# A graph layer whose table rows come by indirect gathers: row fetches per group 16 to 22, two kinds of loads moved from SyncE to ScalarE, the table's end and one buffer moved forward

## The chip, the cores and the metric

The kernel runs on one core of a Trainium2 chip. Its metric is the device time of one execution in microseconds (us). Before the change three runs took 2118.93, 2115.63 and 2113.80 us, median 2115.63. The profile comes from one more execution, which took 2117.82 us.

## The reference

N = 12500 nodes with D = 128 features, E = 212500 edges sorted by destination, 8 heads of 16. Per edge, rows of two projections of the source node are multiplied with a projection of the destination node and with a projection of the edge's attributes:

```python
Q = (x @ WQ).reshape(N, H, dh); K = (x @ WK).reshape(N, H, dh); V = (x @ WV).reshape(N, H, dh)
Eh = (edge_attr @ WE).reshape(-1, H, dh)
score = K[src] * Q[dst] / jnp.sqrt(jnp.float32(dh)) * Eh
score = jnp.exp(jnp.clip(score.sum(-1, keepdims=True), -5.0, 5.0))
wV = jax.ops.segment_sum(V[src] * score, dst, num_segments=N)
Z = jax.ops.segment_sum(score, dst, num_segments=N)
h = x + (wV / (Z + ATTN_EPS)).reshape(N, D)
...
x = _layernorm(x + batchnorm(h) * bn_gamma + bn_beta)   # in the reference spelled out
```

## The kernel before, in words

**Tiles and groups.** The edges are cut into 1661 tiles of 128. A *window* is 4 tiles and a *group* is two windows, 8 tiles; there are 208 groups, and the last one has 5 tiles. One pass of the main loop (line 783) is called iteration g below. It finishes group g and prepares the groups up to g+5.

**The table.** `kvd` in DRAM holds a row of 256 floats (K and V side by side, 1 KB) for every node. `table_rows` (line 669) computes it in 25 steps of 4 blocks of 128 nodes: TensorE multiplies, ScalarE and VectorE take turns at copying out of PSUM, SyncE stores. Groups 0 to 7 do not use the table. Their rows of `x` are gathered (64 gathers) while the table is built and are projected by TensorE: groups 0 to 2 during the table, groups 3 to 7 in `project_main` (line 493), one in each of iterations 2 to 6. From group 8 on, GpSimd gathers the rows of `kvd`, one indirect DMA for each tile (line 225). The first of these waits until the whole table is stored.

**Steps beside the table.** `steps` (line 701) is a list written out by hand that hands work of the first groups out over the table's steps, from step 8 on. Its last entries, `ehqe(0)`, `both_halves(0)`, `turn_back(0)`, `q_mm(2)`, `q_hi(2)` and `q_mid(2)`, fall on the table's steps 21 to 23. `ehqe` multiplies the edge attributes (TensorE, copied out by ScalarE) and spreads Q over the edges (TensorE); `both` multiplies the two (VectorE); `turn_back` transposes the product so that edges lie on the partitions.

**Slots.** A *slot* is 8 KB in each partition and holds one group's table rows. Slots 0 to 7 exist from the start: 0 to 3 first hold x rows of two groups each, 4 to 6 hold the projected rows of groups 0 to 2. A ninth slot (NSLOT) is made at the end of iteration 7 (lines 832 to 836), when the pool `table` (four buffers of 4 KB by partition, line 495 and line 670) is closed. When `message(g)` has read a slot it is free, and `load_kv` (line 279) puts the next group's gathers into `queued`; they are issued in the next iteration, the first of them after TensorE's step of that iteration (`pace`, line 236). So from group 17 on, group k's gathers wait for iteration k-9 at the earliest.

**Rows by SyncE.** In some groups the eighth tile is not gathered by GpSimd. SyncE fetches its 128 rows one at a time: `fetch_rows` (line 268) loads the byte offsets into registers (line 270, one load for all of the iteration's rows) and issues one 1 KB DMA per row (line 277). `ROW_STREAMS` says 16 rows an iteration, from iteration 8 to 199; `row_plan` (line 58) turns that into 24 groups (18, 26, 34, ... 202), each used three iterations after its last row was issued. Such a group has 7 gathers in place of 8.

**What else SyncE issues**, in program order at the start of each iteration: `load(g+4)` (line 490), the edge attributes `ea`, 512 KB, three buffers; below group 16 `load_rel` (line 401), two DMAs of edge places turned along the free axis, one set for each group; from group 16 on `load_quad` (line 388), two DMAs `rbq` of 256 KB for four groups at once, every fourth iteration; then the rows. ScalarE issues only the loads at the start and the stores of turned places (line 380), which `place` makes for 64 windows at a time.

**Who waits for whom among direct DMAs.** The trace's records of SyncE's and ScalarE's direct DMAs show that each carries one of eight semaphores (numbers 100 to 105, 107 and 118), handed round in the program's order over both engines, and that each waits on its own semaphore before it is issued: DMA number n waits until DMA number n-8 has landed, whichever of the two engines issued that one.

**ScalarE in one iteration**, in order: `clip_exp(g)` (lines 607 and 608), `q_hi`, `x_out`, `sums_out`, `q_window`, the two copies of `ehqe(g+2)` (line 562), `q_mid(g+3)` (line 550). After that it waits for the next group's scores.

Of the kernel before, what the change touches and what calls it, by code (L numbers as in the profile page):

```python
# [8 lines left out]
F32 = mybir.dt.float32  # L9
# [8 lines left out]
P = 128  # L18
# [3 lines left out]
G = 8  # L22
U = 4
WN = 64
CH = 512
NSLOT = 8
# [3 lines left out]
ROWS = P  # L30
FIRST_ROW = 8
ROW_LAG = 3
ROW_STREAMS = (("SP", 16),)
RQ = 4


# [46 lines left out]
def gnn_kernel(  # L83
# [19 lines left out]
    nc = tc.nc  # L103
# [3 lines left out]
    usizes, ustarts, cuts, due, _ = plan(N, T)  # L107
    NG = NW // 2
# [8 lines left out]
    rows = ctx.enter_context(tc.tile_pool(name="rows", bufs=1))  # L117
# [5 lines left out]
    tab = tps.enter_context(tc.tile_pool(name="table", bufs=1))  # L123
    late = []
# [85 lines left out]
    free = list(range(NSLOT))  # L210
    pending = list(range(nxg, NG))
# [1 line left out]
    steady = [False]  # L213

    def slot(i):
        return (rows if i < NSLOT else late[0]).tile([P, 2 * G * P], F32, name=f"slot{i}")

    def kv_view(g, t):
        SLOT[g] = t[0]
# [9 lines left out]
    queued = []  # L229
# [18 lines left out]
    for (_, n), groups in zip(ROW_STREAMS, row_plan(usizes)):  # L248
# [6 lines left out]
        if tot % n:  # L255
            q = tot // n
# [22 lines left out]
    def load_kv():  # L279
        while free and pending and table[0]:  # L280
            g = pending.pop(0)
            i = free.pop(0)
            kv_view(g, (i, slot(i)))
            for j in range(sizes[g] - (g in by_row)):
                queued.append((gather, KV[g](j, j + 1, 0, 2 * P).rearrange("p a d -> p (a d)"), kvd,
                               starts[g] + j))
            if not steady[0]:
                issue()

    for g in range(nxg):  # L290
        if g % 2 == 0:
            PAIR[g // 2] = free.pop(0)
            t = slot(PAIR[g // 2])
# [41 lines left out]
    def within(f, g):  # L335
        return f(g) if 0 <= g < NG else None
# [47 lines left out]
    def load_quad(q):  # L384
        t = late[0].tile([P, RQ, U * P], BF16, name="rbq", bufs=2)
        for h in (0, 1):
            at = ustarts[2 * RQ * q + h] * P
            nc.sync.dma_start(t[h * WN:(h + 1) * WN], bass.AP(
                tensor=relT.tensor, offset=relT.offset + at, ap=[[0, WN], [G * P, RQ], [1, U * P]]))
        for k in range(RQ):  # L390
            RB[RQ * q + k] = t[:, k, :]

    quads = range(-(-2 * FIRST_ROW // RQ), sizes.count(G) // RQ)
# [90 lines left out]
    def halves(g):  # L484
        return [(0, usizes[2 * g]), (usizes[2 * g], nt(g))]

    def load(g):
        n = nt(g)
        EA[g] = wp.tile([P, G, P], F32, name="ea", bufs=3)
        nc.sync.dma_start(EA[g][:, :n, :].rearrange("p a b -> p (a b)"),  # L490
                          eaT[:, starts[g] * P:(starts[g] + n) * P])

    def project_main(g):

        half = [tab.tile([P, 4, 2 * P], F32, name="t", bufs=4) for _ in range(2)]
        KV[g] = lambda a, b, c, n=P: half[a // 4][:, a % 4:a % 4 + b - a, c:c + n]
        turn_x(g, 0, True)
        turn_x(g, 4, True)
        yield
        for a in (0, 4):  # L500
            project(g, a, lambda: turned().rearrange("p (a b) d -> p a (b d)", b=2), True)
            yield
# [36 lines left out]
    def q_mm(g):  # L539
        PQ[g] = small_ps[:, 0, :]  # L540
        return nc.tensor.matmul(PQ[g], XW[g], w_q, start=True, stop=True)  # L541

    def q_hi(g):
        Q3[g] = wp.tile([P, 3, P], BF16, name="q3", bufs=2)
        nc.scalar.activation(Q3[g][:, 0, :], PQ[g], AF.Copy, scale=0.25)

    def q_mid(g):
        QR[g] = wp.tile([P, P], F32, name="qr", bufs=1)
        nc.vector.scalar_tensor_tensor(QR[g], PQ[g], 0.25, Q3[g][:, 0, :], op0=OP.mult, op1=OP.subtract)
        nc.scalar.activation(Q3[g][:, 1, :], QR[g], AF.Copy)  # L550
# [4 lines left out]
    def ehqe(g):  # L555

        QE[g], WT[g] = [], []
        for a, b in halves(g):
            eh = psp.tile([P, U * P], F32, name="ps_e", bufs=2)[:, :(b - a) * P]
            nc.tensor.matmul(eh, w_e, EA[g][:, a:b, :].rearrange("p a b -> p (a b)"), start=True, stop=True)  # L560
            t = wp.tile([P, U * P], F32, name="wt", bufs=2)
            nc.scalar.activation(t[:, :(b - a) * P], eh, AF.Copy)  # L562
            WT[g].append(t)
            QE[g].append(psp.tile([P, U * P], F32, name="ps_q", bufs=2)[:, :(b - a) * P])
        for k in range(3):
            for h, (a, b) in enumerate(halves(g)):
                r = slice(h * WN, (h + 1) * WN)
                nc.tensor.matmul(QE[g][h], Q3[g][r, k, :], OT[g][r, :(b - a) * P], start=(k == 0), stop=(k == 2))  # L568
# [6 lines left out]
    def turn_back(g):  # L575

        PW[g] = []
        for h, (a, b) in enumerate(halves(g)):
            ps = turned()
            for j in range(b - a):  # L580
                nc.tensor.transpose(ps[:, j, :], WT[g][h][:, j * P:(j + 1) * P], ident)  # L581
            PW[g].append(ps)
# [84 lines left out]
    NB = -(-N // P)  # L667

    def table_rows(b):
        t = tab.tile([P, 4, 2 * P], F32, name="t", bufs=4)  # L670
        for q in range(b, min(b + 4, NB), 2):
            ps = wide()
            m = min(2, NB - q)
            for i in range(m):
                n = min(P, N - (q + i) * P)
                nc.tensor.matmul(ps[:n, i, :], hx[:, (q + i) * P:(q + i) * P + n], w_kv, start=True, stop=True)
            fl = min(m, N // P - q)
            if fl:
                step = evac(t[:, q - b:q - b + fl, :], ps[:, :fl, :])
            if fl < m:  # L680
                nc.vector.tensor_copy(t[:n, q - b + fl, :], ps[:n, fl, :])
        full = min(4, N // P - b)
        if full > 0:
            nc.sync.dma_start(kvd[b * P:(b + full) * P, :].rearrange("(c p) d -> p c d", p=P), t[:, :full, :])
        if b + 4 > N // P and N % P:
            r0 = N // P * P
            nc.sync.dma_start(kvd[r0:N, :], t[:N - r0, N // P - b, :])
        while len(queued) > max(0, nxg * G - 11 - 12 * (b // 4 + 1) // 5):
            pace(step)

    NQ = -(-NB // 4)
# [4 lines left out]
    def both_halves(g):  # L696
        both(g, 0)
        both(g, 1)
# [2 lines left out]
    steps = [[(locate,)], [(place, runs[0])], [], [(q_mm, 0), (q_hi, 0)],  # L701
             [(q_mid, 0), (load_rel, 0)], [(q_lo, 0), (load, 0)], [(q_mm, 1), (q_hi, 1), (load_rel, 1)],
             [(q_mid, 1)], [(q_lo, 1), (load_rel, 2)], [(load, 1)], [(turned_onehot, 0)],
             [(turned_onehot, 1)], [], [(ehqe, 0), (both_halves, 0)], [(turn_back, 0), (q_mm, 2), (q_hi, 2)],
             [(q_mid, 2)]]
    first_step = NQ - len(steps) - 1
    assert first_step > 3 and max(piece) < first_step + 14
    windows = {first_step + 2: (0, 1), first_step + 8: (2,)}
    for q in range(NQ):
# [5 lines left out]
        for g, a in piece.get(q, []):  # L715
            if a == 0:
                i = free.pop(0)
# [11 lines left out]
        f(*a)  # L729
    table[0] = True  # L730
    load_kv()
    ehqe(1)
    onehot(0)
    within(load, 2)
# [2 lines left out]
    q_window(3)  # L737
    load_rel(4)
    load(3)


    done = set()
# [38 lines left out]
        attn(g)  # L781

    for g in range(NG - 2):
        within(load, g + 4)
        within(load_rel, g + 5)
        if (g + 6) % RQ == 0 and (g + 6) // RQ in quads:
            load_quad((g + 6) // RQ)
        fetch_rows(g)
        within(products, g)
        within(both_halves, g + 1)  # L790
        step = within(add_x, g - 3)
        step = within(q_mm, g + 3) or step
        if step is not None and queued and g >= FIRST_ROW:
            pace(step)
        issue()
        within(gather_sum, g - 1)
        if g + 1 < nxg and g + 1 not in SLOT:
            for _ in project_main(g + 1):
                pass
        within(turn_back, g + 1)  # L800
        within(scores, g)
        within(clip_exp, g)
        within(q_hi, g + 3)
        within(x_out, g - 3)
        within(sums_out, g - 1)
        within(q_lo, g + 2)
        within(denom, g - 2)
        within(recip, g - 2)
        within(attn, g - 2)
        within(q_window, g + 4)  # L810
        within(turned_onehot, g + 3)
        within(ehqe, g + 2)
        within(q_mid, g + 3)
        within(message, g)
        within(onehot, g + 1)
        if g == 2:
            load_last()
        for r in runs[1:]:
            if g == max(4, r[0] // 2 - 12):
                place(r)  # L820
        within_checks(g)
        if NSLOT in free and not pending:
            free.remove(NSLOT)
        while free and todo and not pending:
            load_x()
        bn_parts(2 * g - 5, 2 * g - 3)
        if g == NG - 5:
            assert done >= set(range(NPRE))
            norm_first()
        if g == 4:  # L830
            nc.vector.tensor_scalar(row_ids, row_ids, 8 * P, None, op0=OP.mult)
        if g == FIRST_ROW - 1:
            tps.close()
            late.append(tps.enter_context(tc.tile_pool(name="late", bufs=1)))
            free.append(NSLOT)
            load_kv()
    last = NG - 1
# [327 lines left out]
```

## Time and profile before

| | before |
|---|---|
| runs, median (lowest to highest), us | 2115.63 (2113.80 to 2118.93) |
| profiled execution, us | 2117.82 |
| its span, from first to last instruction, us | 2116.0 |
| what lies around the span, us | 1.8 |
| busy: TensorE, VectorE, ScalarE, GpSimd | 80%, 77%, 30%, 75% |
| gathers of x and of the table on GpSimd | 64 and 1573 |
| rows fetched by SyncE | 3072 |
| bytes moved, mean rate | 386.83 MB, 183 GB/s |

The busy shares are averages over the whole span. [...] SyncE has no busy share at all, since issuing DMAs is not counted; its time is read from the timeline of its own queue. A line of the timeline gives the start, the time from the first to the last instruction of the merged row, the engine (SPq is SyncE's queue), line, operation, tiles, how many, and in brackets how long the engine stood idle before and who ended that.

### The profile page before, as it was taken

Reading aid. Unit: us, or ns where it says so; the run is one execution under the profiler, and the core shown is the slowest. Engines: PE = TensorE matmul, PEld = TensorE weight load, DVE = VectorE, ACT = ScalarE, POOL = GpSimd, SP = SyncE. Lnnn points to the kernel's source line nnn. Section 1 sums busy time; section 2 is a strip of 40 time slices with the busy share of each in tenths; the row PEclk is TensorE's granted clock in tenths of the full one; section 3 lists DMA queues with packets and bytes.
Section 4 is the critical chain, followed back from the end, with each engine's and each line's share of the span. In section 5 each row is a group of like instructions: output and inputs, shape, how many; then the busy total and the mean of one; then the engine's idle time right before and its main releaser. Section 6 shows DMA issues by size and latency. Waiting matters only on the chain. (4 is left out here: it accounts for less than half of the span.)

```text
span 2116.0 us, 37688 instructions
## 1 busy us (share of the span) xinstructions
PE 1694.3 (80%) x9414; PEld 1103.1 (52%) x9414; DVE 1633.9 (77%) x3601; ACT 635.2 (30%) x2480; POOL 1581.2 (75%) x1673
## 2 busy tenths in 40 slices
PE   8899888887777777787877787878787788787877
PEld 6565555555454445455554554455455455454557
DVE  3559989997787787787777777777777778778777
ACT  2343333332232232222222232322222223223225
POOL 7776777777777777777777777777777777777775
PEclk9999999999999998999999999988999998999989
DMA  8856656666566555566565566565566555564674
GB/s 295 289 184 177 187 175 191 188 190 193 158 187 186 167 175 169 157 187 188 167 180 162 159 186 188 168 178 163 165 186 181 176 172 161 168 189 144 184 264 128
DMA packets 177913, 386.83 MB, mean 183 GB/s; under 512 B 38862, under 2 KB 94711, under 8 KB 177687
## 3 DMA queue, kind: packets, MB, share of 16 engines
q0 software_dynamic: 77552, 210.48, 33.9%
q1 hardware_dynamic: 95972, 171.08, 26.5%
q10 hardware_dynamic: 4163, 2.79, 0.4%
q8 instruction: 77, 1.26, 0.2%
q14 instruction: 149, 1.22, 0.2%
HBM read 364.58 MB, written 19.63 MB: 182 GB/s over the span
## 5 line engine op out<-in xcount | busy, mean ns | idle before, releaser
L225 POOL DMA_INDIRECT slot<-kvd,srcs x1573 | 1492.4, 949 | 487.5 <-issue 414.5
L631 PE MATMUL ps_a<-msg,oh 128*128 128x136 f32 (+1 forms) x3322 | 553.1, 308 | 1.7 <-DVE msg L616 1.7
L592 DVE TENSOR_TENSOR p<-slot,ps_t 128x512 f32<-128x512 f32 (+1 forms) x406 | 267.9, 673 | 323.6 <-DMA slot<-kvd,srcs 250.1
L631 PEld LDWEIGHTS ps_a<-msg,oh 128*128 128x128 f32 (+1 forms) x3322 | 447.6, 177 | 86.3 <-issue 61.7
L560 PE MATMUL ps_e<-ea,w_e 128*128 128x512 f32 x832 | 438.8, 654 | 27.7 <-DMA ea<-eaT 26.0
L607 ACT ACTIVATE ps_m<-s 128x64 f32<-128x64 f32 (+1 forms) x209 | 47.5, 227 | 1243.7 <-DVE s L606 931.4
L581 PE MATMUL ps_t<-ident,wt 128*128 128x128 f32 x1661 | 251.2, 293 | 118.0 <-DVE wt L573 116.4
L656 PE MATMUL ps_m<-ident,at 128*128 128x128 f32 x412 | 97.7, 320 | 227.8 <-DVE oh L524 222.9
L581 PEld LDWEIGHTS ps_t<-ident,wt 128*128 128x128 f32 x1661 | 196.3, 148 | 150.5 <-DVE wt L573 143.1
L573 DVE TENSOR_TENSOR wt<-wt,ps_q 128x512 f32<-128x512 f32 x416 | 265.6, 680 | 8.4 <-PE ps_q L568 7.2
L562 ACT ACTIVATE wt<-ps_e 128x512 f32<-128x512 f32 x416 | 233.5, 586 | 65.7 <-PE ps_e L560 61.8
L598 DVE TENSOR_REDUCE s<-p 128x64 f32<-128x1024 f32 (+1 forms) x209 | 251.9, 1205 | 0.1
L616 DVE TENSOR_TENSOR msg<-slot,ps_m 128x1024 f32<-128x1024 f32 (+1 forms) x205 | 242.2, 1182 | 1.4 <-ACT ps_m L607 1.0
L560 PEld LDWEIGHTS ps_e<-ea,w_e 128*128 128x128 f32 x832 | 158.9, 212 | 149.3 <-issue 110.7
L656 PEld LDWEIGHTS ps_m<-ident,at 128*128 128x128 f32 x412 | 63.6, 194 | 319.7 <-ACT q L550 297.1
L568 PE MATMUL ps_q<-ot,q 64*128 64x512 bf16 x1248 | 174.0, 385 | 0.0
L568 PEld LDWEIGHTS <-q 64*128 64x128 bf16 x1248 | 44.5, 95 | 196.7 <-issue 172.6
L521 DVE TENSOR_TENSOR oh<-ps_m,rel_i 128x512 f32<-128x512 f32 x208 | 142.0, 683 | 0.0
L510 ACT ACTIVATE xw<-hx 128x64 f32 x416 | 83.9, 248 | 66.4 <-issue 53.2
L661 ACT ACTIVATE hx<-ps_m 128x64 f32 x412 | 90.4, 219 | 8.0 <-PE ps_m L657 1.2
L647 DVE SCALAR_TENSOR_TENSOR at<-os,keep,rz 128x128 f32<-128x128 f32 x208 | 73.2, 352 | 25.1 <-PE ps_m L656 1.5
L541 PE MATMUL ps_m<-w_q,xw 128*128 128x128 f32 x416 | 86.2, 291 | 1.0 <-ACT xw L510 0.9
(172 smaller groups left out, 1553.7 us busy)
## 6 DMA issues: line engine op xcount, KB each, us to landing
ea<-eaT SPq DMA_DIRECT2D x207, 512.0 KB
byrow<-kvd SPq DMA_DIRECT2D x3072, 1.0 KB
slot<-kvd,srcs POOLq DMA_INDIRECT x1573
rbq<-relT SPq DMA_DIRECT2D x94, 256.0 KB
kvd<-t SPq DMA_DIRECT2D x24, 512.0 KB
slot<-xT SPq DMA_DIRECT2D x24, 256.0 KB
out<-o SPq DMA_DIRECT2D x23, 256.0 KB
hx<-xT SPq DMA_DIRECT2D x11, 512.0 KB
```

The costliest lines, as they stand in the source:

```text
L225: return nc.gpsimd.indirect_dma_start(out=out, out_offset=None, in_=table, in_offset=bass.IndirectOffsetOnAxis(ap=srcs[:, e:e + 1], axis=0))
L521: nc.vector.tensor_tensor(one, iota_ps[:, None, :].to_broadcast([P, n, P]), r[:, :n, None].to_broadcast([P, n, P]), op=OP.is_equal)
L560: nc.tensor.matmul(eh, w_e, EA[g][:, a:b, :].rearrange("p a b -> p (a b)"), start=True, stop=True)
L562: nc.scalar.activation(t[:, :(b - a) * P], eh, AF.Copy)
L568: nc.tensor.matmul(QE[g][h], Q3[g][r, k, :], OT[g][r, :(b - a) * P], start=(k == 0), stop=(k == 2))
L573: nc.vector.tensor_tensor(t, t, QE[g][h], op=OP.mult)
L581: nc.tensor.transpose(ps[:, j, :], WT[g][h][:, j * P:(j + 1) * P], ident)
L592: nc.vector.tensor_tensor(PR[g][:, c:d, :], KV[g](c, d, 0), PW[g][i][:, c - a:d - a, :], op=OP.mult)
L598: nc.vector.tensor_reduce(SS[g][:, a:b, :], PR[g][:, a:b, :].rearrange("p t (h d) -> p t h d", d=DH), axis=AX.X, op=OP.add)
L616: nc.vector.tensor_tensor(MSG[g][:, a:b, :P].rearrange("p t (h d) -> p t h d", d=DH), KV[g](a, b, P).rearrange("p t (h d) -> p t h d", d=D ...
L631: nc.tensor.matmul(AGG[g][WN if j >= n else 0:], OH[g][j], MSG[g][:, j, :], start=(j == 0), stop=(j == n - 1))
L656: nc.tensor.matmul(ps, AT[g], ident, start=True, stop=False)
```

## The change

`ROW_STREAMS` goes from 16 to 22 rows an iteration. SyncE no longer issues `ea` and `rbq` in the loop: ScalarE does, at the end of its work in iteration g, for group g+5 and one iteration earlier for the quads; SyncE loads group 4 ahead of the loop. The steps of group 0 and the Q of group 2 are taken out of the table's steps and stand behind the table. The ninth slot is made at the start and serves as two of the table's four buffers; it is freed for gathers at the end of iteration 6 in place of 7. The first gathers of iterations 8 to 11 no longer wait for TensorE's step.

```diff
-ROW_STREAMS = (("SP", 16),)
+ROW_STREAMS = (("SP", 22),)
...
-        return (rows if i < NSLOT else late[0]).tile([P, 2 * G * P], F32, name=f"slot{i}")
+        return rows.tile([P, 2 * G * P], F32, name=f"slot{i}")
+
+    first = slot(NSLOT).rearrange("p (h c d) -> p h c d", h=2, d=2 * P)
+
+    def table_tile(q):
+        return first[:, q % 4] if q % 4 < 2 else tab.tile([P, 4, 2 * P], F32, name="t", bufs=2)
...
-            nc.sync.dma_start(t[h * WN:(h + 1) * WN], bass.AP(
+            nc.scalar.dma_start(t[h * WN:(h + 1) * WN], bass.AP(
...
-    def load(g):
+    def load(g, by=nc.sync):
...
-        nc.sync.dma_start(EA[g][:, :n, :].rearrange("p a b -> p (a b)"),
+        by.dma_start(EA[g][:, :n, :].rearrange("p a b -> p (a b)"),
...
-        half = [tab.tile([P, 4, 2 * P], F32, name="t", bufs=4) for _ in range(2)]
+        half = [table_tile(2 * (g % 2) + a) for a in (0, 1)]
...
-        t = tab.tile([P, 4, 2 * P], F32, name="t", bufs=4)
+        t = table_tile(b // 4)
...
-             [(turned_onehot, 1)], [], [(ehqe, 0), (both_halves, 0)], [(turn_back, 0), (q_mm, 2), (q_hi, 2)],
-             [(q_mid, 2)]]
-    first_step = NQ - len(steps) - 1
+             [(turned_onehot, 1)]]
+    first_step = NQ - len(steps) - 5
...
     load_kv()
+    ehqe(0)
+    q_mm(2)
+    q_hi(2)
+    both_halves(0)
+    q_mid(2)
+    turn_back(0)
     ehqe(1)
...
     load(3)
+    load(4)
...
     for g in range(NG - 2):
-        within(load, g + 4)
         within(load_rel, g + 5)
-        if (g + 6) % RQ == 0 and (g + 6) // RQ in quads:
-            load_quad((g + 6) // RQ)
         fetch_rows(g)
...
-        if step is not None and queued and g >= FIRST_ROW:
+        if step is not None and queued and g >= FIRST_ROW + 4:
             pace(step)
...
         within(q_mid, g + 3)
+        if g + 5 < NG:
+            load(g + 5, nc.scalar)
+        if (g + 7) % RQ == 0 and (g + 7) // RQ in quads:
+            load_quad((g + 7) // RQ)
         within(message, g)
...
-        if NSLOT in free and not pending:
-            free.remove(NSLOT)
...
             late.append(tps.enter_context(tc.tile_pool(name="late", bufs=1)))
+        if g == FIRST_ROW - 2:
             free.append(NSLOT)
             load_kv()
```

## The prediction

> **What bounds the kernel now.** I read the page's groups first. All sums are made against the profiled execution (2117.82 us: span 2116.0 and 1.8 around it), which lies 2.2 us above the median of the runs, 2115.63.
>
> ```profile
> L225 POOL DMA_INDIRECT slot<-kvd,srcs x1573 | 1492.4, 949 | 487.5 <-issue 414.5
> L592 DVE TENSOR_TENSOR p<-slot,ps_t 128x512 f32<-128x512 f32 (+1 forms) x406 | 267.9, 673 | 323.6 <-DMA slot<-kvd,srcs 250.1
> ```
>
> A gather takes 0.95 us and 0.30 us pass before the next, so GpSimd is occupied without pause, and VectorE waits 250 us in all for gathered rows. The timeline of GpSimd shows the only two pauses up to the last gather:
>
> ```profile
> 82.31 0.94 POOL L225 DMA_INDIRECT slot<-x,srcs  x1 [0.30 <-DVE t L681]
> 86.61 0.94 POOL L225 DMA_INDIRECT slot<-kvd,srcs  x1 [3.36 <-issue]
> ...
> 165.33 0.95 POOL L225 DMA_INDIRECT slot<-kvd,srcs  x1 [0.30 <-issue]
> 171.62 0.94 POOL L225 DMA_INDIRECT slot<-kvd,srcs  x1 [5.34 <-PE ps_m L541]
> ```
>
> At 83 us it waits 3.06 us beyond the usual 0.30 for the stored table, at 166 us 5.04 us for the ninth slot. From group 16's first gather (171.62) to the last (2062.19) there are 1508 steps: 1.2537 us each. Compute starts 77 us behind the gathers (scores of group 8 at 172.60, its last gather at 95.36), needs some 7.6 us a group, has caught up by group 44 and then waits. GpSimd is the bound, and 54 us of tail follow its last gather.
>
> The second chain to know is SyncE's, where nothing else holds it back:
>
> ```profile
> 220.63 1.26 SPq L388 DMA_DIRECT2D rbq<-relT  x2
> 223.46 7.23 SPq L277 DMA_DIRECT2D byrow<-kvd  x16
> 230.79 0.37 SPq L490 DMA_DIRECT2D ea<-eaT  x1
> 232.49 5.13 SPq L277 DMA_DIRECT2D byrow<-kvd  x16
> ...
> 251.99 0.37 SPq L490 DMA_DIRECT2D ea<-eaT  x1
> 252.45 1.25 SPq L388 DMA_DIRECT2D rbq<-relT  x2
> ```
>
> Four iterations take 252.45 - 220.63 = 31.8 us, 7.96 each. A plain one is: load of 16 offsets 1.19, 0.12 to the first row, 16 rows at 0.33 (0.32 undisturbed), 0.05, `ea` 0.41: 7.05. One with a quad takes 10.7, because rows wait for the quad's landing:
>
> ```profile
> SPq L490 <- PE ps_e L560: 209.7, 79, 11.1
> SPq L277 <- DMA relT<-relrow: 161.2, 11, 27.6
> SPq L277 <- DMA rbq<-relT: 99.8, 93, 2.3
> ```
>
> The last two rows are the rule of the eight shared semaphores: a row waits for the DMA eight places earlier, also one that ScalarE issues (`relT`, up to 27.6 us). 3 x 7.05 + 10.7 = 31.85 gives the trace's 31.8, so I trust this sum.
>
> **The change, part by part.**
>
> *Rows.* 22 in place of 16 for 192 iterations (8 to 199) serve 33 groups in place of 24: 1564 gathers, 9 fewer, -11.3 us at 1.2537. Nine more groups split their products and messages by one VectorE row of 0.28 us each; VectorE's waiting hides that.
>
> *The table's end.* TensorE runs without pause from 63 to 82 us. Taking `ehqe(0)` (72.61 to 75.17), `turn_back(0)` and `q_mm(2)` (77.06 to 78.15) out brings the last table rows forward by 3.65 us; the last store goes out at 78.5 in place of 82.20, and 4.41 us later, as now (82.20 to 86.61), gathers could start: 82.95, before the gathers of x end at 83.25. The first pause goes, but by 0.6 us only. The moved steps run behind the table, TensorE's and VectorE's own work beside each other as before; I set them at nothing, between -1 and +2. In return SyncE's loads for groups 2 and 3 go out 3.65 us earlier, and this wait should shrink:
>
> ```profile
> 89.81 0.36 DVE L531 TENSOR_SCALAR ot<-rb,wiota 128x512 bf16<-128x512 bf16 x1 [2.37 <-DMA rb<-relT]
> ```
>
> Compute is then 0 to 2.4 us earlier up to iteration 8.
>
> *The ninth slot.* It is free when group 6's message ends (161.5 now), before GpSimd asks for it. Group 16 now is a row group: 71 gathers from 83.55 end at 172.3. What is late next is group 8's message, whose slot group 17 needs: it ends at 175.40 + 1.21 = 176.6 now, 174.2 to 176.6 after; I take 175. Today group 17 starts at 181.6. From there 1493 gathers x 1.2537 in place of 1501: 181.6 - 175 + 10.0 = 16.6 us earlier. For groups 20 to 24 the wait for TensorE's step returns while compute is held by SyncE (below), one or two microseconds: 15 us are left, with bounds of 10 and 18.
>
> *`ea` and `rbq` by ScalarE.* Their issue is 0.36 us an iteration and 1.25 us every fourth. No row shows ScalarE issuing them; its own stores of `relT` took 0.24 to 0.73, SyncE's rows 0.36 and 0.61, and I take the latter. They stand behind `q_mid`, and behind them is queued the next `clip_exp`, for which VectorE's message waits. The cover is ScalarE's wait for scores:
>
> ```profile
> ACT ps_m L607 <- DVE s L606: 931.4, 158, 10.6
> ```
>
> That is 5.9 us on average; after group 8 the shortest gap between `q_mid` and the next exponential is 2.7. So the issue costs nothing, and a wait in front of it costs nothing up to some 4 us. `ea`'s buffer is free by then (its reader's product has just been copied out). But the shared semaphores now couple the two engines: `ea` of iteration g waits until row 15 of that iteration has landed, and SyncE's row 8 of the next waits until `ea` has landed; in a quad iteration it waits for the second `rbq`. SyncE can no longer run ahead.
>
> *SyncE's loop after.* The load of 22 offsets is not in the trace:
>
> ```profile
> L270 SPq TENSOR_LOAD <-row_ids x192: 1155/1196/1489, 170.5 to 2000.6; - x192
> L842 SPq TENSOR_LOAD <-bad_i x1: 458/458/458, 2048.4 to 2048.4; - x1
> ```
>
> 16 values take 1.19 us behind an `ea` issue (0.36) and 1.45 behind a quad's (0.61); one value 0.46, so 0.05 a value. 22 values: 1.19 if more cost nothing, 1.64 in proportion, 1.49 with the slope. The loads behind a longer issue are longer, and now a row (0.23) stands ahead: I take 1.35. Plain iteration: 1.35 + 0.12 + 22 x 0.33 + 0.05 = 8.78. With a quad, row 8 to row 15 takes 2.3, the landing of row 15 1.65 (median of 192 in the semaphore records), 0.1 to ScalarE's issue, and from `ea`'s issue to the second `rbq` landed 7.7 (46 cases now, 7.3 to 8.25 for the middle eight tenths): 11.75. Mean (3 x 8.78 + 11.75) / 4 = 9.52 us an iteration, where a group's gathers take 8 x 1.2537 less one in 5.8, 9.81. SyncE is the faster of the two by 0.29 only, and it starts 77 us behind. Its chain: load of iteration 8 at 170.5 - 2.4, 192 x 9.52 = 1828, 4 us for the `load_rel` pairs in iterations 8 to 10, then group 200 follows at 2000 and six groups at 7.6: exponentials of group 206 at 2046.5. Today they come at 2061.9. This chain too would end 15 us earlier, at the same time as the gathers. Each 0.1 us in the mean iteration moves it by 19 us.
>
> At this place the Trainium skill speaks against the change. Its page "DMA: Bandwidth & Descriptors", section "Issuing engines are not separate DMA queues", says that starting DMAs from several engines saves only the sequencer's time to issue them, and all run on the same 16 DMA engines. The rows agree: the move frees SyncE of 0.41 + 1.3 / 4 = 0.73 us an iteration, and the waits for landings stay; six more rows and offsets cost 2.1.
>
> **Sum.** Both chains come out 15 us earlier, the tail follows them: 2115.6 - 15 = 2100.6, rounded to 2101.
>
> **The rivals.**
>
> *SyncE and ScalarE in lockstep become the bound (the other side).* Place: row 8 and `ea` as above. From a mean iteration of 9.60 us on, the kernel is no faster than now (2061.9 - 46 - 172 = 1844, over 192). At 9.70 it is 19 us slower than now, 2135; at 9.8, 2154. The Trainium skill's rule, same page and section, would make this the outcome: issue time is all that the move saves. For it: 9.52 is close to 9.60; a load of 1.65 us alone gives 9.75, and a second `rbq` landing 0.5 us later 9.65. Against it: with `ea` and `rbq` on another queue the first rows no longer line up behind them (rows 1 to 5 now land after 2 us, and after 4 behind a quad), and the sum gave the present loop within 0.1. Chances: 0.07 for 9.53 to 9.57 (7 to 14 us faster), 0.09 for 9.57 to 9.63, 0.24 above.
>
> *A wait in place of the ninth slot's.* Compute, held at SyncE's pace from iteration 8, frees slots too late for groups 18 to 30, and GpSimd pauses by 5 to 10 us in all: 2105 to 2112. Iterations 8 to 10 carry 25 to 27 direct DMAs and last 10 to 12 us. Chance 0.10, of which 0.02 lies within 0.3%.
>
> *The table isn't stored earlier* (the last stores land later because more of them are in flight): the first pause stays, but group 17 waits for group 8's message anyway, so only 0 to 2 us are lost. It is inside the forecast's bounds.
>
> **How the numbers follow.** Forecast 0.50 (10 to 18 us faster). Faster by over 0.3%, which is 6.3 us and about what a measurement can tell from no change: 0.50 + 0.07 + 0.08 = 0.65; within: 0.09 + 0.02 = 0.11; slower 0.24. The range goes from 2094 (the forecast's better bound, and a run-to-run share of 3 us) to 2136 (the lockstep at 9.70); some 0.12 lies above and 0.04 below.
>
> **What would show it.** 1564 gathers and 4224 rows. No pause at 83 us, first gather of the table near 83.6; group 17's first gather at 174 to 177; no later pause of GpSimd over 2 us. SyncE's time from one quad to the next near 38.1 us for four iterations, loads of about 1.35 us. ScalarE waiting for `byrow` landings ahead of line 490, without VectorE waiting longer for ScalarE. Group 206's scores at 2045. The prediction is wrong if four iterations of SyncE take over 38.4 us, or if VectorE, late in the kernel, waits for ScalarE instead of gathers.

## The result, and the profile after

The changed kernel takes **2800.31 us** (median of five runs, 2792.37 to 2802.93) against 2115.63 us before (five runs, 2113.80 to 2118.93): a ratio of 1.3232, 95% interval 1.3217 to 1.3246. The forecast was 2101 us, faster; it is 32% slower, far outside the range. The profiled execution took 2802.93 us, its span is 2801.1.

Ten of the eighteen runs below fell on three other chips, on which the kernel before itself takes 2723 to 2793 us; there only ratios to the kernel before on the same chip are used, and the last section shows what differs.

The change does at the start what it says. GpSimd's timeline, with the idle time ahead of a gather in brackets (0.30 is the usual):

```profile
83.74 0.94 POOL L230 DMA_INDIRECT slot<-kvd,srcs  x1 [0.77 <-DMA rb<-relT]
...
174.41 0.94 POOL L230 DMA_INDIRECT slot<-kvd,srcs  x1 [2.13 <-DVE msg L621]
...
705.50 0.94 POOL L230 DMA_INDIRECT slot<-kvd,srcs  x1 [16.49 <-PE ps_m L546]
```

The table's first gather stands at 83.74 and group 17's at 174.41, as forecast. But from 253 us on GpSimd stops again and again, about once for every group that takes a tile by row, for 6 to 38 us. The groups say what happened to the bound. VectorE's products by row before, where they waited 5.3 us in all for SyncE's rows:

```profile
L592 DVE TENSOR_TENSOR p<-byrow,ps_t 128x128 f32<-128x128 f32 x24 | 6.8, 281 | 5.3 <-DMA byrow<-kvd 5.3
```

And after, with GpSimd's gathers:

```profile
L230 POOL DMA_INDIRECT slot<-kvd,srcs x1564 | 1480.5, 947 | 1094.8 <-PE ps_m L546 609.5
...
L597 DVE TENSOR_TENSOR p<-byrow,ps_t 128x128 f32<-128x128 f32 x33 | 9.5, 288 | 958.2 <-DMA byrow<-kvd 958.2
```

The gathers themselves cost what they did (947 ns each), but GpSimd's idle time rose from 487.5 to 1094.8 us, because the first gather of an iteration waits for TensorE's step, and that comes late. And VectorE, which waited for gathers before, now waits **958 us for SyncE's rows**: 33 products, 29 us ahead of each. SyncE has become the bound. The granted TensorE clock, 0.81 in place of 0.93, is not what slows it: TensorE's matmuls take no longer (`ps_a` 293 ns in place of 308, `ps_e` 645 in place of 654), and its busy time fell from 1694 to 1622 us. The chain of what ended last has SyncE's queue beside the compute, in shares of the span (SPq is SyncE's queue):

```profile
DVE 29%; SPq 29%; PE 14%; DMA 12%; issue 11%; POOL 2%; ACT 2%; DVEq 1%; ACTq 0%; POOLq 0%
```

What SyncE waits for (total us, times, longest), and its loads of 22 offsets (shortest, median, longest in ns):

```profile
SPq L282 <- DMA ea<-eaT: 391.1, 134, 7.0
SPq L282 <- DMA rbq<-relT: 155.7, 70, 9.5
```

```profile
L275 SPq TENSOR_LOAD <-row_ids x192: 1861/1947/5197, 166.4 to 2696.2; - x192
```

SyncE's rows wait 547 us for transfers that it no longer issues. The loads' median is 1.95 us, not 1.35. They are of two kinds: 1.92 us in iterations 8 to 135, and 4.88 us from iteration 136 on, where the list's second block of columns begins, 88 bytes further on.

From the first load to the last, SyncE's mean iteration is (2696.2 - 166.4) / 191 = **13.24 us**, where 9.52 was forecast. Split by the trace's records over iterations 28 to 135: rows 5.72, gaps between them 1.51, load 1.93, other idle time 0.12, so 9.28 us of its own, and waits for `ea` 2.39 and for `rbq` 0.93. Together that is 12.6.

**Work and compute take turns.** The two lines below, from SyncE's timeline, are each 88 rows in four iterations; the third is GpSimd's pause in the same stretch:

```profile
1400.99 34.83 SPq L282 DMA_DIRECT2D byrow<-kvd  x88
...
1438.20 59.92 SPq L282 DMA_DIRECT2D byrow<-kvd  x88
```

```profile
1447.33 0.94 POOL L230 DMA_INDIRECT slot<-kvd,srcs  x1 [38.12 <-PE ps_m L546]
```

From load to load these are 9.3 us an iteration while compute stands still, and 15.5 once compute runs again (an exponential every 7.5 us from 1442.3 on). An earlier stretch, starts of SyncE's loads (by iteration) and of the exponentials (by group), in us:

```
loads         49: 698.3   50: 714.8   51: 732.9   52: 744.7   53: 754.7   54: 763.8   55: 773.1
exponentials  51: 700.3   52: 707.9   53: 717.8   54: 726.0   55: 734.0   56: 742.0   57: 773.7
```

While groups 51 to 55 run at some 8 us each, SyncE's iterations 49 and 50 take 16.5 and 18.1 us. Then group 57, which needs a tile by row, comes 31.7 us after group 56, and in that time SyncE does three iterations at 9 to 10 us. Whichever of the two runs, the other is held back.

The records of the semaphores say why. The order in which the eight shared semaphores are handed round is not the order in which the code stands. The `ea` that ScalarE issues in iteration 25 comes, in the round of its semaphore, between rows that SyncE issues in iterations 21 and 22; that of iteration 16 between rows of 13.7 and 14.4 (14.4 is four tenths of the way through iteration 14's rows); that of 57 between rows of 54.6 and 55.2. SyncE's rows of iteration i therefore wait for an `ea` that ScalarE issues two to four iterations later, while compute waits, three iterations after, for those same rows. In the kernel before, where SyncE issued both, every `ea` stood half an iteration from its rows. But ScalarE's few stores of `relT` were out of place there already: the first of the two that it issues at the end of iterations 20, 52 and 84 stands between rows of 17.8 and 18.4, 49.8 and 50.4, 81.8 and 82.4. So what stands ahead of the prediction under "Who waits for whom among direct DMAs", that the semaphores are handed round in the program's order over both engines, does not hold.

### The profile page after: what moved, and what is told of

Same layout as the page of the kernel before. It is cut to its first block, busy times and chain, and to the rows that moved or that the text cites. A ratio compares the mean times of both kernels' runs of the same rounds, so it can differ in the third digit from the quotient of the medians.

```text
span 2801.1 us, 39907 instructions
## 1 busy us (share of the span) xinstructions
PE 1621.7 (58%) x9414; PEld 1070.6 (38%) x9414; DVE 1621.4 (58%) x3619; ACT 642.1 (23%) x2480; POOL 1569.1 (56%) x1664
## 3 DMA queue, kind: packets, MB, share of 16 engines
q8 instruction: 77, 1.26, 0.2%
## 4 chain that ended last, share of the span: by engine, by line
DVE 29%; SPq 29%; PE 14%; DMA 12%; issue 11%; POOL 2%; ACT 2%; DVEq 1%; ACTq 0%; POOLq 0%
SPq L282 19%; SPq L275 10%; DVE wt L578 5%; DVE msg L621 5%; DVE s L603 5%; DMA ea<-eaT 5%; PE ps_a L636 4%; DVE p L597 3%; PE ps_e L565 3%; DVE oh L526 3%; DMA rbq<-relT 2%; POOL slot L230 2%; DMA byrow<-kvd 2%; DMA slot<-kvd,srcs 2%; PE ps_t L586 2%
## 5 line engine op out<-in xcount | busy, mean ns | idle before, releaser
L230 POOL DMA_INDIRECT slot<-kvd,srcs x1564 | 1480.5, 947 | 1094.8 <-PE ps_m L546 609.5
L586 PEld LDWEIGHTS ps_t<-ident,wt 128*128 128x128 f32 x1661 | 210.4, 154 | 964.5 <-DVE wt L578 958.8
L597 DVE TENSOR_TENSOR p<-byrow,ps_t 128x128 f32<-128x128 f32 x33 | 9.5, 288 | 958.2 <-DMA byrow<-kvd 958.2
L636 PE MATMUL ps_a<-msg,oh 128*128 128x136 f32 (+1 forms) x3322 | 515.0, 293 | 1.0 <-DVE msg L621 0.8
L636 PEld LDWEIGHTS ps_a<-msg,oh 128*128 128x128 f32 (+1 forms) x3322 | 413.9, 166 | 80.1 <-issue 52.0
L565 PE MATMUL ps_e<-ea,w_e 128*128 128x512 f32 x832 | 431.9, 645 | 0.7 <-ACT wt L567 0.7
L597 DVE TENSOR_TENSOR p<-slot,ps_t 128x512 f32<-128x512 f32 (+1 forms) x410 | 256.7, 667 | 0.4 <-issue 0.2
L567 ACT ACTIVATE wt<-ps_e 128x512 f32<-128x512 f32 x416 | 240.3, 588 | 41.4 <-PE ps_e L565 30.5
L621 DVE TENSOR_TENSOR msg<-slot,ps_m 128x1024 f32<-128x1024 f32 (+3 forms) x209 | 243.7, 1168 | 0.4 <-ACT ps_m L612 0.3
```

The lines of the kernel that those rows point to most:

```text
L230: return nc.gpsimd.indirect_dma_start(out=out, out_offset=None, in_=table, in_offset=bass.IndirectOffsetOnAxis(ap=srcs[:, e:e + 1], axis=0))
L597: nc.vector.tensor_tensor(PR[g][:, c:d, :], KV[g](c, d, 0), PW[g][i][:, c - a:d - a, :], op=OP.mult)
L621: nc.vector.tensor_tensor(MSG[g][:, a:b, :P].rearrange("p t (h d) -> p t h d", d=DH), KV[g](a, b, P).rearrange("p t (h d) -> p t h d", d=D ...
L636: nc.tensor.matmul(AGG[g][WN if j >= n else 0:], OH[g][j], MSG[g][:, j, :], start=(j == 0), stop=(j == n - 1))
```

## The experiments

**Theory A**: this order makes SyncE's work and the compute take turns, and the longer loads add to it. **Rival B**: 22 rows are simply too much for SyncE, whoever issues the rest. On the three other chips come first the runs that undo parts.

### The list of offsets, aligned

Each iteration's 22 offsets lie in a partition of `row_ids`; the second block of columns starts 128 bytes on, not 88.

```diff
-            at = (q % P, cols + q // P * n, min(n, tot - q * n))
+            at = (q % P, cols + q // P * 32, min(n, tot - q * n))
...
```

> The changed kernel with one edit: the second block of row offsets starts 128 bytes after the first in place of 88, so that every load of 22 offsets starts at a multiple of 32 bytes. Theory A (a load that starts off such a multiple is slow: 1.95 us in the first 128 iterations, 4.87 in the last 64): all loads 1.95, the last 64 iterations 2.9 us shorter each, total about 2613 us. Rival (the late loads are slow for another reason, such as traffic or the registers in use late in the kernel): unchanged, about 2800 us.

("Theory A" there is about the start of the block alone.)

On a chip where the kernel before takes 2776 us: 3462.52 us, one run, 1.247 of it. That says nothing against 2800 on another chip. The same kernel beside the changed one, unedited, on a chip with 2115.16 us before:

> The changed kernel, nothing edited, beside the kernel before on the same chip: where the kernel before takes 2115 us, 2800 us; where it takes 2780 us, its ratio says what the change is worth there. If SyncE's long instructions set the time there, the list that is not aligned adds 2.95 us to 64 iterations: 3463 + 190 = 3650 us.

> The aligned list alone, once more. Where the kernel before takes 2115 us: the changed kernel's 2800 less between 97 us (64 x the 1.5 us by which its last iterations are longer than those before) and 190 us (64 x 2.95 us of load): 2610 to 2705 us under both theories. Where it takes 2780 us: 3463 us again.

Measured: 2809.00 unedited and 2721.70 aligned, one run each. The loads:

```profile
L275 SPq TENSOR_LOAD <-row_ids x192: 1864/1924/2144, 166.5 to 2613.4; - x192
```

No load is over 2.15 us now, so the start of the block made the 4.88. The gain is 87 us: 64 iterations at 14.20 became 12.76, a little under the 97 us estimated, and 2721.70 lies above the stated 2610 to 2705. Only half of the 2.95 us saved in a load reaches the time; the waits for `ea` and `rbq`, 1.86 us in those iterations with the long loads, grow to 3.38. The rest of the loss, 607 us, is elsewhere.

### SyncE issues `ea` and `rbq` again, with 22 and with 16 rows

```diff
-            nc.scalar.dma_start(t[h * WN:(h + 1) * WN], bass.AP(
+            nc.sync.dma_start(t[h * WN:(h + 1) * WN], bass.AP(
...
-            load(g + 5, nc.scalar)
+            load(g + 5)
```

With this alone (and the aligned list), or with 16 rows alone (`ROW_STREAMS = (("SP", 16),)`), or with both:

> As the run with the aligned offsets, and ea and the quads are issued by SyncE again, at the place where ScalarE issued them. Theory A (the eight semaphores shared by the two engines' DMAs make SyncE's rows wait for ea and quads that ScalarE issues later than the rows are ready): these waits, 3.3 us an iteration, go; SyncE's iteration is load 1.95, rows 7.3, ea 0.41, quads 0.9 on average, 10.6 in all, 192 of them, about 2300 us. Rival B (SyncE's rows are simply too many, it makes no difference who issues ea and quads): their issue comes on top, 2613 + 0.73 x 192 = about 2750 us.

> The changed kernel with 16 rows an iteration as before, everything else as changed. Theory A (shared semaphores): SyncE's own work is 6.6 us an iteration, with waits of about 3 us for ea and quads 9.6 to 9.9, so the kernel ends between 2110 and 2180 us, and SyncE waits for ea. Rival B (22 rows are too many): SyncE has 3 us to spare, GpSimd is the bound again and the start's gain of 7 us shows, about 2108 us.

> The changed kernel with 16 rows and with ea and quads issued by SyncE: what is left of the change is the start (table's end, ninth slot, order of the first gathers). Both theories: group 17's gathers start at 174.4 in place of 181.6, nothing else moves, about 2108 us, 7 below the kernel before.

On the chip with 2776 us before: 3232.86 us (one run, ratio 1.165), 3035.82 us (ratio 1.0933, interval 1.0895 to 1.0972) and 2785.63 us (1.0034, 1.0013 to 1.0055). Neither part alone is harmless, and with 16 rows B expected no loss from ScalarE's issuing; but the size can't be carried over. Two were run again on another chip:

> 22 rows with an aligned list of offsets, ea and rbq issued by SyncE again: the kernel of e2_aligned_sync once more. Both theories: slower than before, since SyncE's iteration is its own 9.4 us of before, less the 0.8 us for which it waits for TensorE there, plus 6 x 0.325 for rows and 0.7 for the longer load: 11.2 to 12.1 us, 192 of them and 306 us around them give 2456 to 2630 us. Theory A: every ea stands in the order of its semaphore within one iteration of the rows beside it, as before. Rival B expects it slower than the changed kernel with the aligned list.

> The changed kernel with 16 rows a group as before, ScalarE still issuing ea and rbq: the kernel of e3_rows16 once more, beside a kernel before that should take some 2115 us. Theory A (the eight shared semaphores tie SyncE's rows to ScalarE's transfers of about four iterations later, and ROW_LAG gives only three): still clearly slower than before, 1.05 to 1.12 of it (2220 to 2370 us). Rival B (22 rows are simply too many for SyncE): 0.995 to 1.005 of before.

There the kernel before takes 2784.73 us; ratios 1.1686 (1.1658 to 1.1714) and 1.0959 (1.0928 to 1.0991): the same again. Then on chips with 2115 us:

> 16 rows, ea and rbq by ScalarE, once more. Where the kernel before takes 2115 us: theory A 2220 to 2370 us, rival B 2105 to 2125 us. Where it takes 2780 us: 3040 us again.

> 22 rows with the aligned list, ea and rbq issued by SyncE as before: no semaphore order between SyncE and ScalarE. Where the kernel before takes 2115 us: theory A 306 + 192 x 10.3 to 12.1 = 2284 to 2630 us, below g1_aligned's 2722; rival B 2722 us or more, as SyncE now issues more.

> 16 rows, ea and rbq by SyncE: of the change only the new start is left (table's last rows ahead of the first group's steps, ninth slot early, one load ahead). Both theories: the first pause of GpSimd (3.06 us) and most of the second (5.04 us, of which 2 are left) go: 2108 us, 6 to 8 us under the kernel before; a ratio of 0.996 to 0.998.

Measured: 2296.02, 2310.65 (one run each, both in A's ranges) and 2109.71 us (ten runs, beside 2114.66 before; ratio 0.9974, 0.9964 to 0.9983). In one table (the second block of offsets starts at byte 64 with 16 rows, at byte 128 with 22):

| | SyncE issues `ea`, `rbq` | ScalarE does |
|---|---|---|
| 16 rows | 2109.71 | 2296.02 |
| 22 rows | 2310.65 | 2721.70 |

Both are right in part. 22 rows cost 201 us with SyncE issuing, which is B: its mean iteration is 10.66 us there, and TensorE waits 434 us for `ea`, VectorE 113 us for rows. ScalarE's issuing, meant to relieve SyncE, costs 186 us at 16 rows and 411 at 22, which B has no reason for. With 16 rows and ScalarE, VectorE's wait for rows is there again:

```profile
L597 DVE TENSOR_TENSOR p<-byrow,ps_t 128x128 f32<-128x128 f32 x24 | 6.9, 287 | 492.3 <-DMA byrow<-kvd 492.3
```

`h_sync16` keeps only the new start, and is the version that beats both kernels: GpSimd's two pauses shrink to 0.43 and 1.22 us beyond the usual 0.30, from 3.06 and 5.04, 6.4 us in all. A new one at 678 us, 1.2 us beyond the usual, gives some back, and the time falls by 5.0.

```profile
83.80 0.94 POOL L230 DMA_INDIRECT slot<-kvd,srcs  x1 [0.73 <-issue]
...
175.23 0.94 POOL L230 DMA_INDIRECT slot<-kvd,srcs  x1 [1.52 <-DVE msg L621]
```

### Rows used later

If SyncE must be four iterations behind, let the compute use the rows later:

```diff
-ROW_LAG = 3
+ROW_LAG = 5
```

> The changed kernel with the aligned list and one constant changed: a group that takes a tile by row is used five iterations after its last row is issued, not three (ROW_LAG 5). Not one row, load or transfer is saved. Theory A: SyncE may now be four iterations behind ScalarE without making VectorE wait, so its work runs beside the compute again and its own 9.3 to 9.8 us an iteration sets the time: 306 + 192 x 9.3 to 9.8 = 2092 to 2190 us. Rival B: 22 rows cost what they cost, 2600 to 2700 us.

> As f5_aligned_lag5 with 20 rows a group. Theory A: SyncE's iteration falls by 2 x 0.325 = 0.65 us to 8.7 to 9.1, below the pace of the gathers, and GpSimd sets the time again: 2095 to 2115 us. Rival B: about 2450 to 2550 us.

On the chip with 2784.73 us before: 3463.22 us (1.2439, 1.2412 to 1.2466), which is the 1.247 of the aligned list alone, and 3264.74 us with 20 rows (1.1742, 1.1712 to 1.1772). And with 2115.16 us before:

> The kernel of f5_aligned_lag5 once more (aligned list, ROW_LAG 5). Where the kernel before takes 2115 us: theory A 2092 to 2190 us, rival B 2600 to 2700 us. Where it takes 2780 us: 3463 us again, since SyncE's own work sets the time there.

2719.49 us, one run: **no gain, A's forecast missed by 530 us.** Theory A in this form falls. The trace says why: the order moved with the constant. The `ea` of iteration 25 now stands between rows of 20.2 and 20.8 (21.1 and 22.0 before), that of 65 between 60.6 and 61.2. The order reads as if SyncE were placed as far behind as the use of its rows allows, so a later use buys nothing; that is a reading of the two orders, not more. VectorE still waits 855.7 us for rows. A remains possible only if the order itself is changed.

### One wait more, to change the order alone

```diff
...
+    def tie(dma, g):
+        if g in ROW:
+            tc.add_manual_dep(dma.ins, ROW[g].ins.name,
+                              mybir.DependencyInfo(mybir.DependencyClass.Sync, mybir.DependencyReason.DATA),
+                              reason="tie")
...
-                nc.sync.dma_start(by_row[k][r % P:r % P + 1, 0, :].bitcast(U8), kvb[ds(off, 8 * P)].unsqueeze(0))
+                ROW[g] = nc.sync.dma_start(by_row[k][r % P:r % P + 1, 0, :].bitcast(U8),
+                                           kvb[ds(off, 8 * P)].unsqueeze(0))
...
-        by.dma_start(EA[g][:, :n, :].rearrange("p a b -> p (a b)"),
-                          eaT[:, starts[g] * P:(starts[g] + n) * P])
+        tie(by.dma_start(EA[g][:, :n, :].rearrange("p a b -> p (a b)"),
+                         eaT[:, starts[g] * P:(starts[g] + n) * P]), g - 6)
```

The `ea` that ScalarE issues in iteration g also waits for the last row of iteration g-1. Nothing is taken away.

> The aligned list of g1_aligned, and one wait added: ScalarE's ea of an iteration also waits for the last row of the iteration before. Nothing is saved; the wait brings every ea and rbq to within one iteration of the rows beside it in the order of the shared semaphores, where SyncE's rows stood three to seven iterations behind. Where the kernel before takes 2115 us: theory A (the order of the semaphores makes SyncE's work and the compute take turns) 306 + 192 x 9.3 to 10.5 = 2092 to 2322 us, far under g1_aligned's 2722, though a wait was only added. Rival B (SyncE's 22 rows, or the transfers, are what takes the time): 2722 us or more, since ScalarE now waits besides. Where the kernel before takes 2780 us: 3460 us under both.

> As h_tied22 with 16 rows a group (the list's blocks still 128 bytes apart). Where the kernel before takes 2115 us: theory A: SyncE's iteration is 16 x 0.325 + 1.3 + 0.3 = 6.8 us and some waiting, under the pace of the gathers, so 2100 to 2180 us against 2296 without the wait; rival B (ScalarE's issuing itself delays the compute): 2296 us or more.

Beside 2114.66 us before, one run each: **2431.71 us** with 22 rows, 290 less than without the wait, and **2113.21 us** with 16, 183 less. B expected no gain. The `ea` of iteration 25 now stands between rows of 24.6 and 25.2, and so it goes through the loop (the expectation puts SyncE three to seven iterations behind, which was too much: the rows that wait for an `ea` are two to four behind, and four to six with ROW_LAG 5). VectorE's wait ahead of products by row is gone. ScalarE waits for SyncE's rows instead, 601 us in 66 places with 22 rows, before `ea`: compute is held at SyncE's pace, in step with it. VectorE's row among the groups, and SyncE's waits, 22 rows:

```profile
L605 DVE TENSOR_TENSOR p<-byrow,ps_t 128x128 f32<-128x128 f32 x33 | 9.2, 279 | 0.0
```

```profile
SPq L289 <- DMA ea<-eaT: 229.4, 190, 4.6
SPq L289 <- DMA rbq<-relT: 137.0, 94, 2.4
```

Two waits of 650 us in all (with the aligned list alone: 472.7 and 177.7) became 366. Under A the added wait should gain, and it does; that ScalarE's issuing itself delays the compute, B's reason at 16 rows, is ruled out by the 2113.21. The wait changes the order and also holds ScalarE back, and this edit cannot part the two; but `h_sync16` has the near order without such a wait and takes about the same time (2109.71 us), and VectorE's wait for rows is 7.5 us there, where it is 492.3 with ScalarE issuing and no added wait. So the order is the cause of the turns. It is not all: 2432 is 110 us above the top of what A expected, since in this order SyncE still waits 1.2 us an iteration for `ea` (`ea` is issued 1.67 us after the last row, once that row has landed, and lands 3.93 after that, 5.6 in all by the medians; meanwhile SyncE has only a load of 1.92 and eight rows of 0.325 to do, 4.5).

### A number of rows in between

> As h_tied16 with 18 rows a group: 27 groups take a tile by row, 3 gathers fewer (3.8 us). Theory A: SyncE's own work is 18 x 0.325 + 1.4 + 0.25 = 7.5 us an iteration and some 2 us of waiting for landings, 9.5, just under the 9.8 that a group's gathers take, so GpSimd still sets the time: 2105 to 2112 us. If the waiting stays at h_tied16's 2.7, 10.2 us an iteration and SyncE sets it: 2130 to 2250 us.

> As h_sync16 with 18 rows a group and blocks 128 bytes apart. SyncE's iteration grows by 2 x 0.325 and 0.2 of load from 9.4, of which 0.7 is waiting that it can give up: 9.55, beside GpSimd's 9.8: 2104 to 2108 us if it holds, 1 to 5 us under h_sync16; 2115 to 2130 us if SyncE becomes the bound.

They fell on a chip with 2736.57 us before: 2735.93 us (1.0001, 0.9974 to 1.0027) and 2888.92 us (1.0552, 1.0524 to 1.0579). There SyncE is the bound, as the last section shows, and the tied order carries two rows more than the kernel before in the same time; whether it beats 2109.71 us on a chip with 2115 us stays open.

## Why the prediction was wrong, point by point

**What bounds the kernel now**: right. `h_sync16`, 6.4 us less pause at the start, is 5.0 us faster.

**Rows, table's end, ninth slot**: right where they could show. 1564 gathers and 4224 rows; 83.74 us against 83.6 forecast, 174.41 in 174.2 to 176.6. The 9 gathers' 11 us are saved on GpSimd and buried.

**"So the issue costs nothing"** (ScalarE): right as to the issue. `h_tied16`, where ScalarE issues and waits besides, is within 4 us of `h_sync16`.

**The step that failed is SyncE's loop after**, in three terms.

- *"`ea` of iteration g waits until row 15 of that iteration has landed, and SyncE's row 8 of the next waits until `ea` has landed."* That took the order of the code for the order of the semaphores. For `ea` and `rbq` the trace of before could not tell them apart: there SyncE issued them and the rows, so one engine's order was the order. For ScalarE's `relT` stores it could: they stand more than two iterations ahead of their place in the code, and the prediction's own line for them, 161.2 us in 11 waits of up to 27.6, is the price (seven waits of 12 to 27.6 us, one for each such place). The prediction read the rule of the eight semaphores from that line, but not the order. With two engines the rounds are laid out as if SyncE ran several iterations behind; what lays them out so was not looked into. Waits forecast: 11.75 - 8.78 = 2.97 in a quad iteration, 0.74 a mean iteration. Measured with the aligned list: 472.7 + 177.7 = 650 us, 3.4 an iteration. In `h_tied22`, close to the order that the prediction assumed, the `rbq` term is right: 137.0 / 192 = 0.71.
- *"I take 1.35"* for the load of 22 offsets. It is 1.92, above the upper bound of 1.64 that came from 16 values in 1.19, and 4.88 where the block starts at byte 88. The bounds assumed a price by the number of values; where the list lies was not in the rows of before, whose blocks of 16 values were 64 bytes each.
- *Own work of 8.78 us.* It is 9.28; the load alone is 0.57 more, the rest slightly less than forecast.

**The price of a longer iteration** was right: "Each 0.1 us in the mean iteration moves it by 19 us." By 2101 + 192 x (mean - 9.52):

| | mean iteration, us | by this formula | measured |
|---|---|---|---|
| changed kernel, profiled | 13.24 | 2815 | 2802.93 |
| `g1_aligned` | 12.81 | 2733 | 2721.70 |
| `h_tied22` | 11.29 | 2441 | 2431.71 |
| `h_sync22` | 10.66 | 2320 | 2310.65 |
| `g3_rows16` | 10.60 | 2308 | 2296.02 |

So the 699 us between 2101 and 2800 are, by this account: for the block at byte 88, 87 (2809.00 - 2721.70); the turns, 290 (2721.70 - 2431.71); the load's 0.57 us, 109 (192 x 0.57); the wait for `ea` that `h_tied22` keeps, 230 (192 x 1.2). That is 716, 17 more than there are: the formula that prices the last two is itself some 10 us high, and the 2809.00 of the single run beside `g1_aligned` is 9 above 2800.31.

**The rivals.** The one on the other side, lockstep as the bound, came true in kind. Its place (rows and `ea` waiting for each other through shared semaphores) was right; its mechanism is that of `h_tied22`, not that of the changed kernel, where the two do not step together but take turns. Its price was held near break-even by 9.52; the load alone, at its measured 1.92, would have made 10.1 of it and 2210 us. Of the others, the table was stored in time (0.47 us beyond the usual ahead of 83.74), and slots freed too late for groups 18 to 30 can't be told apart in the changed kernel, where GpSimd stops from 253 us on for SyncE's rows. The Trainium skill ("DMA: Bandwidth & Descriptors", section "Issuing engines are not separate DMA queues") says that another issuing engine saves issue time only. The runs agree that no more was to be had, and go further: at 22 rows the move did not save, it cost 411 us.

**What would have shown it** did: "wrong if four iterations of SyncE take over 38.4 us" (they take 51 to 57), and the waits for landings, not the issue, are what SyncE's queue shows.

## What to carry to other kernels

DMAs of two engines that share a round of semaphores are tied in the order in which the semaphores are handed out, which need not be the order of the code; when an issue moves to another engine, read from the records beside which instructions each transfer stands (a few transfers that the other engine already issues, as `relT` here, can show it before the change is made), and one dependency that pulls it back can be worth far more than it costs. A queue with 3% of slack is the bound of the next version: price every added instruction on it from a row with the same size and place, and take a long range where there is none. Undo the parts one at a time, in both settings of the other part: here the two losses together (612 us) are more than their sum (387).

## What the runs showed that was not expected

**Where a block of register values lies.** A load of 22 values from SBUF took 1.86 to 1.92 us with the block at byte 0 or 128 of the row and 4.88 at byte 88; 16 values took 1.20 to 1.26 with the second block at byte 64. Which boundary counts was not tried.

**The same kernel on other chips.** On three chips the kernel before took 2723 to 2793 us in place of 2115. The traces there differ from the others in SyncE's queue. The two kinds of instruction of a row (shortest, median, longest in ns), in `h_sync16` and in the same kernel on such a chip, `e4_rows16_sync`:

```profile
L282 SPq MOVE byrow<-kvd x3072: 29/29/38, 170.1 to 2002.0; - x192
L282 SPq DMA_DIRECT2D byrow<-kvd x3072: 218/228/317, 170.2 to 2002.1; - x192
```

```profile
L282 SPq MOVE byrow<-kvd x3072: 2/29/1407, 253.2 to 2690.8; - x192
L282 SPq DMA_DIRECT2D byrow<-kvd x3072: 2/228/1475, 253.3 to 2690.8; - x192
```

The medians agree, but on such a chip some 400 of the 3072 register moves take about 0.7 us, in clusters, nearly one an iteration, with gaps of the same length between instructions; SyncE's mean iteration from 28 to 135 is 12.7 us there and 9.4 in `h_sync16`, and the rows begin some 83 us later. Fewer of the DMAs' semaphore events are in that trace too (some 9,800 in place of 39,300). What causes it was not found; it makes SyncE the bound of every version traced there, so what a version gains by GpSimd cannot be seen there.
